# Pair sums from the third block, the short block added to a pair, and a new ScalarE order at the start: one change to a fused four-layer graph network

## The chip, the cores and the metric

The kernel runs on one core of one Trainium2 chip. The metric is the device time of one execution in microseconds; the time given for a kernel is the median of its runs. A change of about 0.2% (6.5 us) is what a measurement of this kernel can tell from no change.

## The reference, cut to what matters

Four graph layers run one after the other on 2708 nodes with 512 features, each with a residual and a layer norm. The change touches layer 0 and the beginning of layer 1:

```python
# layer 0: N = 2708, H = 4 heads of D = 128; both masks are the same adj here
Xw = einsum('hnd,hde->hne', Xh, W)                 # values
f1 = einsum('hnd,hd->hn', Xw, V[:, 0, :, 0]); f2 = einsum('hnd,hd->hn', Xw, V[:, 1, :, 0])
sig = sigmoid(f1[:, :, None] + f2[:, None, :])
att = masked_softmax(adj * sig, adj != 0)          # per row, per head
Xn  = batchnorm(att @ Xw)                          # first attention pass
emb = batchnorm(elu(Xn @ enc_W.T + b) + Xn)
Y   = elu((att @ emb) @ W.T)                       # second attention pass
out = batchnorm(elu(Y @ dec_W.T + b) + Y)
x = layernorm(x + out)
# layer 1
hidden = x @ W1 + b1
x = layernorm(x + (adj != 0) @ hidden / deg)
```

## The kernel before, in words

The nodes are cut into `NT` = 22 blocks of 128 rows; the last one has 20. Python code builds the program once; a tile framework puts the instructions of each engine (TensorE is PE in the profile, VectorE DVE, ScalarE ACT, GpSimd POOL, SyncE SP) into one list, in the order of their priorities and of the framework's own estimate of when each can start. `tc.issue_after(ins)` gives the instructions under it a place behind `ins` in that order. On the chip each engine works through its list in order, and semaphores hold an instruction until its inputs and its buffer are ready. DMAs are issued by SP (`nc.sync`), POOL (`nc.gpsimd`) and ACT (`nc.scalar`), each in the order of its list too.

**First attention pass** (`attention_pass` with `first=True`). Two halves of the columns (`HSPAN`, 1354 each) and two pairs of heads give four sets, here called set 0 (half 0, heads 0 and 1), set 1 (half 0, heads 2 and 3), set 2 and set 3 (half 1). In each set the 22 blocks come in the order `ORDER`: 0 to 10, then the short block of 20 rows at place 11, then the other ten. "Block 9" below is the block at place 9 of its set. For each block `form` makes the attention numerators of both heads in one tile `t` of 128 x 2 x 1354:

- `L400` (ACT): tanh of one head's scores, twice; sigmoid is (1 + tanh)/2.
- `L408` (DVE): add and multiply with the mask tile `a`, both heads in one instruction ("the mask").
- `L409` (ACT): exp of both heads.
- `L491` (PE): twelve products of `t` with the values `xw` into six PSUM tiles `po`.
- `L524` (PE): sums of the rows with a tile of ones into `psm`, eight products.

In sets 0 and 2 (`prepare`) the mask tile is also made from the raw adjacency (`L391`, `L392` on DVE) and stored to DRAM as `adj_d` (`L396`, issued by POOL). Some blocks' `t` are stored too, for the second pass (`L473`, POOL, 1354 KB): blocks 4, 8, 11, 14 and 18 of sets 0 and 2, and eight blocks of sets 1 and 3. There are four buffers for `t` and four for `a`, so the tanh of block k + 4 waits for the products (and the store, if any) of block k.

In sets 1 and 3 the row sums are taken of pairs: for the places from `ALONE` = 4 to 19 the even block waits, and at the odd one DVE adds both (`L517`, one add per head, into the tiles tagged `z` and `pair`), so that one group of eight `L524` products serves two blocks. Places 0 to 3, 20 and 21 are alone. The short block at place 11 is paired with block 10 by adding its rows into the first 20 rows of block 10's own `t` (`L509`), which block 10's `L491` products read.

At the end of a set `keep` copies `po` out and sends the row sums through DRAM; the eight `scaled` steps it returns (multiply `L634` and `bn_stats` `L635` each) are issued one per place in the next set, from place 4 on.

**From layer 0 to layer 1.** `decode` ends with the last decoder products (`ps_dec`, `L893`). Meanwhile `centre` has loaded `w1` and the first five of six column chunks of `xT` into the tile `xs`, and subtracted the mean from `w1` in place. Then the batch norm's scale and shift are found (`ready`), DVE copies `w1` out of `xs` (`L1037`) and clears the last block of `hid_hi` (`L1027`), SP loads the sixth chunk into the place where `w1` was, and for each chunk of `CHUNKS` (450 or 452 columns) ACT scales each of the four feature groups (`L1044`) and DVE adds `xT` (`L1051`). For every block of 128 columns that is complete PE makes a transpose (`tp_out`, `L1057`) and the product with `w1` (`ps_hid`, in `L128`).

Of the kernel before, what the change touches and what calls it, by code (L numbers as in the profile page):

```python
# [8 lines left out]
F32 = mybir.dt.float32  # L9
# [8 lines left out]
P = 128  # L18
# [11 lines left out]
def gnn_stack_kernel(  # L30
# [110 lines left out]
    CHUNKS = [(h0 + q0, w) for (h0, _), ch in zip(HSPAN, HCH) for q0, w in ch]  # L141
    NCH = len(CHUNKS)

    SQ = 4
    SW = 2 * ((HW + 2 * SQ - 1) // (2 * SQ))
    SCH = [[(q * SW, min(SW, w - q * SW)) for q in range(SQ)] for _, w in HSPAN]
# [5 lines left out]

    ORDER = list(range(NT // 2)) + [NT - 1] + list(range(NT // 2, NT - 1))

    ALONE, LAST = 4, 2

# [15 lines left out]
    with ExitStack() as l0:  # L174
# [33 lines left out]
        xT_sb = feat_tile("xT_sb")  # L208

        def load_mlp(w, name):  # L210
            t = p0.tile([P, C, F], F32, tag="mlp_w", name=name)
            nc.sync.dma_start(t, w.rearrange("(c p) o -> p c o", p=P))
            return t

        def project(att, psum):

            held = p0.tile([P, C, F], F32, tag="mlp_w", name="held").rearrange("p c f -> p (c f)")
            w0x = held[:, : H * (P + 2)].rearrange("p (h e) -> p h e", h=H)  # L220
            v12 = att.tile([P, H, 2], F32, tag="v12", name="v12", bufs=1)
            nc.sync.dma_start(v12[:, :, 1], v2.rearrange("(h e) -> e h", h=H))
# [115 lines left out]
        def attention_pass(values, first, att, psum, finish, f1b=None, blocks=(), spread=None, rest=None, taken={}):  # L338
# [23 lines left out]
            def form(hf, p, jt, att, prepare, f1b, tv):  # L362

                h0, w = HSPAN[hf]
                j0, n = BLOCKS[jt]
                src = adjT if prepare else adj_d
                if prepare and hf == 0 and jt < len(blocks):
                    a = blocks[jt]
                else:
                    a = att.tile([P, HW], F32, tag="a", name="a", bufs=4 if first else 3)  # L370

                    early = prepare and hf == 0 and jt < len(blocks) + 2
                    with tc.issue_after(spread.ins) if early else nullcontext():
                        loads.append(
                            nc.sync.dma_start(a[:n, :w], src[j0 : j0 + n, h0 : h0 + w])
                        )
                if n < P:

                    for r in range(HB):
                        if r > 0:  # L380
                            nc.sync.dma_start(
                                a[r * Q : r * Q + n, :w], src[j0 : j0 + n, h0 : h0 + w]
                            )
                        if r + 1 < HB:
                            nc.sync.dma_start(
                                a[r * Q + n : (r + 1) * Q, :w], src[: Q - n, h0 : h0 + w]
                            )
                    n = HR
                if prepare:
                    z = att.tile([P, HW], F32, tag="z", name="z", bufs=1)  # L390
                    nc.vector.tensor_scalar(z[:n, :w], a[:n, :w], 0.0, None, ALU.is_equal)  # L391
                    nc.vector.scalar_tensor_tensor(  # L392
                        a[:n, :w], z[:n, :w], -BIG, a[:n, :w], ALU.mult, ALU.add
                    )
                    m = BLOCKS[jt][1]
                    nc.gpsimd.dma_start(adj_d[j0 : j0 + m, h0 : h0 + w], a[:m, :w])  # L396

                for k in range(HP):
                    h = HP * p + k
                    nc.scalar.activation(  # L400
                        tv[:, k, :],
                        f1b[k][:n, :w],
                        AF.Tanh,
                        bias=f2h[:n, jt, h : h + 1],
                        scale=0.5,
                    )
                ab = a[:n, :w].unsqueeze(1).to_broadcast([n, HP, w])
                step = nc.vector.scalar_tensor_tensor(tv, tv, GUARD, ab, ALU.add, ALU.mult)  # L408
                nc.scalar.activation(tv, tv, AF.Exp, scale=0.5)  # L409
                if not first and p == (jt in KEPT[0]):  # L410

                    with tc.issue_after(step.ins):
                        count(hf, jt, att, a)
                return step
# [5 lines left out]

            later = []
            loads = []
            po = None
            for hf, (h0, w) in enumerate(HSPAN):
                for p in range(H // HP):
# [26 lines left out]
                    for place, jt in enumerate(ORDER):  # L452
# [48 lines left out]

                        if prepare or not ALONE <= place < NT - LAST:
                            whole, m = [t[:, k, :] for k in range(HP)], n
                        elif place % 2 == 0:
                            before = t
                            continue
                        elif n < P:
                            whole, m = [before[:, k, :] for k in range(HP)], P
                            nc.vector.tensor_tensor(  # L509
                                before[:n, :, :w], before[:n, :, :w], tv, ALU.add  # L510
                            )
                        else:

                            whole, m = [], P
                            for k, tag in enumerate(("z", "pair")):
# [2 lines left out]
                                    both[:, :w], before[:, k, :w], tv[:, k, :], ALU.add  # L518
                                )
                                whole.append(both)  # L520
                        for k in range(HP):
                            for r, (q0, qw) in enumerate(SCH[hf]):

# [69 lines left out]
        with (  # L593
# [8 lines left out]
            def keep(hf, p, po, sums):  # L602
# [11 lines left out]
                if not final:  # L614
# [12 lines left out]
                    nc.sync.dma_start(rs_d[part].rearrange(wide).rearrange(cut, s=SR), few)  # L627
                    rb = spread_sums(att, hf, p)

                    def scaled(k, r):  # L630
                        h = HP * p + k
                        q0, qw = SCH[hf][r]
                        dst = ft[:, h, h0 + q0 : h0 + q0 + qw]
                        nc.vector.tensor_tensor(dst, dst, rb[:, k, q0 : q0 + qw], ALU.mult)  # L634
                        nc.vector.bn_stats(stats[:, h, SQ * hf + r, :], dst)  # L635

                    return [
                        lambda k=k, r=r: scaled(k, r) for k in range(HP) for r in range(SQ)
                    ]

                sel = att.tile([P, HW], F32, tag="a", name="sel", bufs=4)
# [59 lines left out]
        with (  # L701
# [104 lines left out]
            def centre(pm):  # L806
# [7 lines left out]
                    xs.rearrange("p t f -> p (t f)")[:, C * c0 : C * (c0 + w)].rearrange(  # L814
                        "p (c j) -> p c j", c=C
                    )
                    for c0, w in CHUNKS
                ]
                for ci in early:
                    load_x(x_held, ci)  # L820
# [9 lines left out]


            held1 = {}
            early = [ci for ci, (c0, w) in enumerate(CHUNKS) if C * (c0 + w) <= (NT - C) * F]

            def load_x(x_held, ci):
                c0, w = CHUNKS[ci]
                nc.sync.dma_start(
                    x_held[ci], xT[:, c0 : c0 + w].rearrange("(c p) j -> p c j", p=P)
                )

            def decode(hf, p, po, rb):
# [145 lines left out]
                wk_again = rest[0][:, : C * F].rearrange("p (c o) -> p c o", c=C)  # L987
                wq_again = rest[1][:, : C * P].rearrange("p (c o) -> p c o", c=C)
                mqk = rest[1][:, C * P : C * P + F]
                nc.sync.dma_start(wk_again, wkT_d)  # L990
                nc.sync.dma_start(wq_again, wqT_d)
                with tc.issue_after(last_dec[0].ins):
# [18 lines left out]
        nc.vector.reciprocal(rdeg, dsum)  # L1011
        scale3, mean3 = batch_scale(stats, MG_DEC, "bn3")
        shift3 = batch_shift(scale3, mean3, MBETA_DEC, "bn3")
        xs, w1_held, x_held = held1["xs"], held1["w1"], held1["x"]

    with (
# [4 lines left out]
        hid_hi = p1.tile([P, NT, F], F32R, name="hid_hi")  # L1023
        hid_lo = p1.tile([P, NT, F], F32R, name="hid_lo")

        with tc.issue_after(ready[0].ins):
            nc.vector.memset(hid_hi[:, NT - 1, :].bitcast(F32), 0.0)  # L1027

# [1 line left out]
        work = main.enter_context(tc.tile_pool(name="l1w", bufs=2))  # L1032
        with tc.tile_pool(name="l1a", bufs=1) as pre:
            b1_sb = load_row(pre, b1, "b1_sb")
            w1_sb = pre.tile([P, C, F], F32, name="w1_sb")
            with tc.issue_after(ready[0].ins):
                nc.vector.tensor_copy(w1_sb, w1_held)  # L1037
            for ci in range(len(early), NCH):
                load_x(x_held, ci)
            turned = 0  # L1040
            for ci, (c0, w) in enumerate(CHUNKS):
                for c in range(C):
                    cols = ot[:, c, c0 : c0 + w]
                    nc.scalar.activation(  # L1044
# [775 lines left out]
```

## Time and profile before

| | |
|---|---|
| time, median of 3 runs | 3248.69 us (3248.22 to 3251.64) |
| the profiled execution's own time | 3254.93 us |
| its span, first to last instruction | 3253.1 us |
| busy: PE, DVE, ACT, POOL | 99%, 59%, 41%, 4% of the span |
| first attention pass (first `po` to the last) | 42.40 to 556.5 us |
| second attention pass begins | 671.9 us |
| last decoder products of layer 0 end | about 1168 us |
| first `ps_hid` of layer 1 | 1173.65 us |
| costliest groups: L408 DVE, L400 ACT, L491 PE (with `xw`), L409 ACT | 444.5, 411.4, 415.1, 367.5 us busy |

Busy times are shares of the whole span and hide what a stage waits for. A busy PE is modelled from the starts of matmuls, so its idle times and the granted clock (1.00 is full, 0.50 is half) tell more than its share. In a timeline row the numbers are the start, the time taken, the engine, the line, what is written and read, and in brackets the idle time of the engine before it and who ended that.

### The profile page before, as it was taken

To read this page: it belongs to the slowest core of one execution; us is meant where nothing else is said; L and a number is where in the kernel's file an instruction comes from. 1 tells how busy PE (TensorE), PEld (TensorE's weight loads), DVE (VectorE), ACT (ScalarE), POOL (GpSimd) and SP (SyncE) were. 2 spreads that over 40 slices of the span, in tenths; PEclk is the share of its full clock that TensorE was granted. 3 is DMA by queue.
4 is the path that set the end of the run, shared out by engine and by line. 5 is a ranking of instruction groups with operands and counts; after the bars stand their busy time and mean duration, and the time that the engine had idled before them with its cause. 6 is when DMAs were issued, how large, how long until landed. Compare 5 with 4: busy or idle time off the path is not lost.

```text
span 3253.1 us, 30379 instructions
## 1 busy us (share of the span) xinstructions
PE 3210.1 (99%) x10906; PEld 1718.6 (53%) x10906; DVE 1924.7 (59%) x3152; ACT 1317.7 (41%) x1494; POOL 136.3 (4%) x219
## 2 busy tenths in 40 slices
PE   8999999999999999999999999999999999999999
PEld 5444444444444446875555555554555555555554
DVE  7888977767686684444145667776353342542433
ACT  6888886567767552001133434443011020120211
POOL 1100100000000000000010000000000000000000
PEclk9999999999999999999999999999999999999999
DMA  8867764346545413540044444553211111111100
GB/s 286 309 214 256 278 243 157 112 141 242 189 165 202 169 47 97 142 126 8 1 135 127 123 127 136 151 159 103 73 47 32 45 36 35 43 32 46 34 24 20
DMA packets 175030, 399.32 MB, mean 123 GB/s; under 512 B 21242, under 2 KB 115910, under 8 KB 168670
## 3 DMA queue, kind: packets, MB, share of 16 engines
q1 hardware_dynamic: 157950, 314.59, 31.5%
q0 software_dynamic: 16496, 80.70, 6.5%
q8 instruction: 86, 1.41, 0.2%
q10 hardware_dynamic: 432, 2.08, 0.2%
q14 instruction: 66, 0.54, 0.0%
HBM read 315.46 MB, written 81.30 MB: 122 GB/s over the span
## 4 chain that ended last, share of the span: by engine, by line
PE 83%; issue 9%; DVE 3%; ACT 2%; DMA 1%; POOL 1%; SPq 0%; POOLq 0%; DVEq 0%; ACTq 0%
PE po L1385 23%; PE ps_s L1264 18%; PE po L491 15%; PE ps_nb L1117 7%; PE ps_wide L1166 4%; PE ps_hid L128 2%; PE ps_sup L1562 2%; PE ps_o L1493 2%; PE ps_dec L893 2%; PE ps_mlp L768 1%; PE psm L524 1%; ACT t L400 1%; ACT t L409 1%; PE ps_s L1256 1%; DVE t L408 1%
## 5 line engine op out<-in xcount | busy, mean ns | idle before, releaser
L408 DVE SCALAR_TENSOR_TENSOR t<-t,a 128x2708 f32<-128x2708 f32 (+1 forms) x150 | 444.5, 2975 | 154.1 <-ACT t L400 149.4
L400 ACT ACTIVATE t<-f1b,f2h 128x1354 f32<-128x1354 f32 (+1 forms) x300 | 411.4, 1413 | 65.6 <-PE po L491 33.3
L491 PE MATMUL po<-t,xw 128*128 128x452 f32 (+3 forms) x1056 | 415.1, 557 | 7.2 <-ACT t L409 7.2
L1264 PE MATMUL ps_s<-sup,hT 128*128 128x384 f32 (+1 forms) x1176 | 407.4, 490 | 0.0
L1385 PE MATMUL po<-sup,e 128*128 128x512 f32 x882 | 407.1, 595 | 0.0
L409 ACT ACTIVATE t<-t 128x2708 f32<-128x2708 f32 (+1 forms) x150 | 367.5, 2454 | 95.8 <-DVE t L408 95.6
L1385 PE MATMUL po<-e,xs 128*128 128x384 f32 (+1 forms) x1176 | 406.0, 489 | 0.0
L491 PE MATMUL po<-t,emb 128*128 128x452 f32 (+3 forms) x1056 | 397.1, 545 | 3.8 <-ACT t L409 3.8
L1696 DVE SCALAR_TENSOR_TENSOR e<-a_cols,ps_s 128x384 f32<-128x384 f32 (+1 forms) x154 | 85.5, 555 | 451.0 <-PE ps_s L1264 428.0
L1264 PEld LDWEIGHTS ps_s<-sup,hT 128*128 128x128 f32 x1176 | 221.8, 190 | 164.2 <-issue 14.2
L491 PEld LDWEIGHTS po<-t,xw 128*128 128x128 f32 (+1 forms) x1056 | 191.0, 192 | 220.0 <-issue 195.6
L1385 PEld LDWEIGHTS po<-e,xs 128*128 128x128 f32 x1176 | 222.2, 190 | 160.2 <-issue 5.8
L491 PEld LDWEIGHTS po<-t,emb 128*128 128x128 f32 (+1 forms) x1056 | 193.6, 190 | 200.3 <-issue 192.1
L1385 PEld LDWEIGHTS po<-sup,e 128*128 128x128 f32 x882 | 160.4, 190 | 159.6 <-issue 136.9
L1264 PE MATMUL ps_s<-hT 128*128 128x384 f32 (+5 forms) x672 | 211.1, 461 | 0.9 <-ACT sup L1569 0.7
L1363 ACT ACTIVATE e<-e 128x384 f32<-128x384 f32 (+1 forms) x308 | 151.7, 522 | 115.0 <-DVE e L1362 111.7
L1611 ACT ACTIVATE a_cols<-a_cols,neg_big 128x384 f32<-128x384 f32 (+1 forms) x154 | 94.6, 616 | 226.5 <-DMA a_cols<-in_adjT_dram 188.2
L1117 PE MATMUL ps_nb<-hid_hi,at 128*128 128x512 f32 x484 | 185.6, 390 | 0.4 <-DVE at L1109 0.4
L1117 PE MATMUL ps_nb<-hid_lo,at 128*128 128x512 f32 x462 | 180.1, 390 | 0.0
L1362 DVE TENSOR_TENSOR e<-e,nmax 128x384 f32<-128x384 f32 (+1 forms) x308 | 162.6, 549 | 23.3 <-ACT nmax L1355 23.3
L108 ACT ACTIVATE ln_rstd<-ln_rstd 128x1 f32<-128x1 f32 (+1 forms) x88 | 17.3, 201 | 392.8 <-DVE ln_rstd L107 392.3
L1264 PEld LDWEIGHTS ps_s<-hT 128*128 128x128 f32 x672 | 123.1, 190 | 89.4 <-issue 20.5
(254 smaller groups left out, 3322.5 us busy)
## 6 DMA issues: line engine op xcount, KB each, us to landing
a<-adj_d SPq DMA_DIRECT2D x108, 677.0 KB
a_cols<-in_adjT_dram SPq DMA_DIRECT2D x378, 192.0 KB
kept<-t POOLq DMA_DIRECT2D x22, 1354.0 KB, 7.3
t<-kept SPq DMA_DIRECT2D x22, 1354.0 KB
a<-in_adjT_dram SPq DMA_DIRECT2D x42, 677.0 KB
adj_d<-a POOLq DMA_DIRECT2D x42, 677.0 KB, 6.0
raw<-in_adjT_dram SPq DMA_DIRECT2D x105, 256.0 KB
a_cols<-in_adjT_dram SPq DMA_DIRECT2D x63, 202.0 KB
```

Source lines behind the costliest of these rows:

```text
L400: nc.scalar.activation(tv[:, k, :], f1b[k][:n, :w], AF.Tanh, bias=f2h[:n, jt, h : h + 1], scale=0.5,)
L408: step = nc.vector.scalar_tensor_tensor(tv, tv, GUARD, ab, ALU.add, ALU.mult)
L409: nc.scalar.activation(tv, tv, AF.Exp, scale=0.5)
L491: nc.tensor.matmul(po[HB * k + q][:, :qw], values[r : r + n, jt, h * P : (h + 1) * P], t[r : r + n, k, q0 : q0 + qw], start=(place == 0), ...
L1117: nc.tensor.matmul(pos[it][:n], at, half[:, jt, :], start=(jt == 0 and k == 0), stop=(jt == NT - 1),)
L1166: nc.tensor.matmul(ps[:, :width], w(c, o), xt(c), start=(c == 0), stop=(c == C - 1),)
L1264: nc.tensor.matmul(ps[:, b * P : w], keys[:, c, j0 : j0 + P], st["q"][:, c, b * P :], start=(c == 0), stop=(c == C - 1),)
L1362: nc.vector.tensor_tensor(e, e, st["nmax"][:, :w], ALU.add)
L1363: nc.scalar.activation(e, e, AF.Exp)
L1385: nc.tensor.matmul(out, lhsT, rhs, start=(k == 0), stop=(k == NT - 1))
L1611: nc.scalar.activation(a, a, AF.Identity, bias=neg_big[: a.shape[0]], scale=1.0e30)
L1696: nc.vector.scalar_tensor_tensor(e, a, 2.0, ps, ALU.mult, ALU.add)
```

## The change

In seven places, all in layer 0 and at the start of layer 1:

1. `ALONE` goes from 4 to 3, so pairs begin at place 3 and blocks 9 and 10 form a pair of their own. The short block at place 11 is added, by one add per head, into the first 20 rows of that pair's sum tiles, and the group's products come then.
2. In the first set, the tanh of the blocks 1 to 4 are put behind a given instruction: those of block 1 behind the last tanh of block 0, those of blocks 2, 3 and 4 behind the exp of blocks 0, 1 and 2.
3. The eight `scaled` steps become sixteen: multiply and `bn_stats` are separate.
4. The pool of the tag `mlp_w` changes from `p0` to `pf`, which stays open until layer 1's inputs are made.
5. `w1` is brought out of `xs` by a DMA from SP behind the last decoder product, into the buffer of `dec_w`, instead of by DVE.
6. The memset of `hid_hi`'s last block is on POOL.
7. The first column chunk is cut into 128 and 324 columns (`PIECES`), for the loads of `xT` and for layer 1's start.

```diff
+    PIECES = [(0, P), (P, CHUNKS[0][1] - P)] + CHUNKS[1:]
...
-    ALONE, LAST = 4, 2
+    ALONE, LAST = 3, 2
+    assert ORDER.index(NT - 1) % 2 == ALONE % 2 == NT % 2 + 1
...
         def load_mlp(w, name):
-            t = p0.tile([P, C, F], F32, tag="mlp_w", name=name)
+            t = pf.tile([P, C, F], F32, tag="mlp_w", name=name)
...
-            held = p0.tile([P, C, F], F32, tag="mlp_w", name="held").rearrange("p c f -> p (c f)")
+            held = pf.tile([P, C, F], F32, tag="mlp_w", name="held").rearrange("p c f -> p (c f)")
...
+                turn = opening.get(jt) if prepare and hf == 0 else None
                 for k in range(HP):
                     h = HP * p + k
-                    nc.scalar.activation(
-                        tv[:, k, :],
-                        f1b[k][:n, :w],
-                        AF.Tanh,
-                        bias=f2h[:n, jt, h : h + 1],
-                        scale=0.5,
-                    )
+                    with tc.issue_after(turn.ins) if turn else nullcontext():
+                        tanh = nc.scalar.activation(
+                            tv[:, k, :],
+                            f1b[k][:n, :w],
+                            AF.Tanh,
+                            bias=f2h[:n, jt, h : h + 1],
+                            scale=0.5,
+                        )
                 ab = a[:n, :w].unsqueeze(1).to_broadcast([n, HP, w])
                 step = nc.vector.scalar_tensor_tensor(tv, tv, GUARD, ab, ALU.add, ALU.mult)
-                nc.scalar.activation(tv, tv, AF.Exp, scale=0.5)
+                exp = nc.scalar.activation(tv, tv, AF.Exp, scale=0.5)
+                if not opening:
+                    opening[1] = tanh
+                if len(opening) < 4:
+                    opening[len(opening) + 1] = exp
...
+            opening = {}
...
                         if prepare or not ALONE <= place < NT - LAST:
                             whole, m = [t[:, k, :] for k in range(HP)], n
-                        elif place % 2 == 0:
+                        elif n < P:
+                            m = P
+                            for k in range(HP):
+                                nc.vector.tensor_tensor(
+                                    whole[k][:n, :w], whole[k][:n, :w], tv[:, k, :], ALU.add
+                                )
+                        elif before is None:
                             before = t
                             continue
-                        elif n < P:
-                            whole, m = [before[:, k, :] for k in range(HP)], P
-                            nc.vector.tensor_tensor(
-                                before[:n, :, :w], before[:n, :, :w], tv, ALU.add
-                            )
                         else:
...
                                 whole.append(both)
+                            before = None
+                            if BLOCKS[ORDER[place + 1]][1] < P:
+                                continue
...
-                    def scaled(k, r):
+                    def scaled(k, r, counted):
...
-                        nc.vector.tensor_tensor(dst, dst, rb[:, k, q0 : q0 + qw], ALU.mult)
-                        nc.vector.bn_stats(stats[:, h, SQ * hf + r, :], dst)
+                        if not counted:
+                            nc.vector.tensor_tensor(dst, dst, rb[:, k, q0 : q0 + qw], ALU.mult)
+                        else:
+                            nc.vector.bn_stats(stats[:, h, SQ * hf + r, :], dst)
...
+                w1_sb = pf.tile([P, C, F], F32, tag="mlp_w", name="w1_sb")
+                with tc.issue_after(last_dec[0].ins):
+                    nc.sync.dma_start(w1_sb, held1["w1"])
+                held1["w1"] = w1_sb
                 nc.sync.dma_start(wk_again, wkT_d)
...
-        with tc.issue_after(ready[0].ins):
-            nc.vector.memset(hid_hi[:, NT - 1, :].bitcast(F32), 0.0)
+        nc.gpsimd.memset(hid_hi[:, NT - 1, :].bitcast(F32), 0.0)
...
-            w1_sb = pre.tile([P, C, F], F32, name="w1_sb")
-            with tc.issue_after(ready[0].ins):
-                nc.vector.tensor_copy(w1_sb, w1_held)
-            for ci in range(len(early), NCH):
+            for ci in range(len(early), len(PIECES)):
                 load_x(x_held, ci)
             turned = 0
-            for ci, (c0, w) in enumerate(CHUNKS):
+            for ci, (c0, w) in enumerate(PIECES):
```

(The two other loops over `CHUNKS` that serve these loads, in `x_held` and `early`, run over `PIECES` as well.)

## The prediction

> **What bounds the kernel now.** I read the page first, then a table by stage, then the timelines of the engines at the places where the stages lose time.
>
> ```profile
> span 3253.1 us, 30379 instructions
> PE 3210.1 (99%) x10906; PEld 1718.6 (53%) x10906; DVE 1924.7 (59%) x3152; ACT 1317.7 (41%) x1494; POOL 136.3 (4%) x219
> ...
> core 0: us, PE busy (x) PEld busy (x) DVE busy (x) ACT busy (x) POOL busy (x), PEclk, DMA share, GB/s
> 42.40:171.98 129.58, 129.58 (x617) 55.99 (x616) 117.78 (x71) 111.18 (x67) 18.03 (x31) 1.00 0.82 289
> 171.98:294.15 122.17, 120.00 (x492) 53.48 (x489) 101.85 (x62) 109.63 (x68) 6.22 (x11) 0.99 0.66 233
> 294.15:432.92 138.77, 134.67 (x620) 57.86 (x617) 122.84 (x89) 115.73 (x70) 15.76 (x28) 0.96 0.79 279
> 432.92:556.50 123.58, 119.79 (x492) 53.91 (x488) 93.89 (x65) 101.12 (x62) 4.93 (x9) 0.99 0.54 189
> ```
>
> TensorE sets the end, so I ask only where it waits or runs slowly. The four rows are sets 0 to 3 of the first attention pass. With no wait an alone block takes 6.03 us (42.40 to 48.43 in the timeline), a pair 10.58 (4.66 and 5.92), and the 20-row block with its sums 2.99. Set 0 is 21 x 6.03 + 2.99 = 129.6: nothing is lost. Sets 1 and 3 should take 117.9 and lose 4.2 and 5.7; set 2 should take 129.6 and loses 9.2. So 19 us lie open in this pass. Where:
>
> ```profile
> 235.77 2.49 PE L524 MATMUL psm<-t,ones 128*32 128x340 f32 x16 [1.41 <-DVE t L509]
> ...
> 357.88 6.51 PE L491 MATMUL po<-t,xw 128*128 128x452 f32 x12 [2.20 <-ACT t L409]
> ...
> 369.62 7.83 PE L491 MATMUL po<-t,xw 128*128 128x452 f32 x12 [0.96 <-ACT t L409]
> ...
> 511.02 9.16 PE L491 MATMUL po<-t,xw 128*128 128x452 f32 x19 [2.38 <-ACT t L409]
> ...
> core 0: us, PE busy (x), PEclk, DMA share, GB/s
> 235.80:239.21 3.41, 3.41 (x18) 0.50 0.02 5
> 358.68:362.09 3.41, 3.41 (x6) 0.50 0.82 278
> 368.92:375.75 6.83, 6.12 (x8) 0.50 0.94 320
> ```
>
> The bracket is TensorE's idle time and who ended it. The second table shows that after such waits the granted clock is 0.50 for 3.41 us or twice that, so a wait also costs up to 1.7 or 3.4 us of slow matmuls.
>
> The wait of 357.88 begins on POOL's queue:
>
> ```profile
> 343.88 0.53 POOL L396 DMA_DIRECT2D adj_d<-a  x1 [5.45 <-DVE a L392]
> 344.40 0.53 POOL L473 DMA_DIRECT2D kept<-t  x1
> ```
>
> The 1354 KB store of block 8's `t` goes out right behind the 677 KB store of `a` and lands 9.5 us later (the DMA issues of this window). The tanh of block 12 needs that buffer and stands ahead of block 10's exp on ScalarE (4.67 us idle there).
>
> The opening and the start of layer 1:
>
> ```profile
> 30.24 8.00 ACT L400 ACTIVATE t<-f1b,f2h 128x1354 f32<-128x1354 f32 x6 [1.71 <-DMA f1b<-f_d]
> 38.14 2.44 ACT L409 ACTIVATE t<-t 128x2708 f32<-128x2708 f32 x1
> ...
> 34.33 2.98 DVE L408 SCALAR_TENSOR_TENSOR t<-t,a 128x2708 f32<-128x2708 f32 x1 [1.85 <-ACT t L400]
> ...
> 1171.37 1.34 PE L1057 MATMUL tp_out<-ident,ot 128*128 128x128 f32 x4 [3.40 <-DVE ot L1051]
> 1173.65 2.08 PE L128 MATMUL ps_hid<-w_sb,ot 128*128 128x512 f32 x2 [0.93 <-DVE w_sb L1037]
> ```
>
> Six tanh run before the first exp, and the first mask (L408) waits for the third, since the two heads of block 0 stand first and third. Layer 1's first product waits for the copy of `w1`.
>
> **The change, part by part** (by the changed program's own instruction order).
>
> *Opening.* ScalarE's list becomes tanh 0,0,1,1, exp 0, tanh 2,2, exp 1, instead of 0,1,0,1,2,2, exp 0. The mask of block 0 starts one tanh (1.32 us, 7.90/6) earlier. The chain of waits there runs 34.33 mask, 37.31 copies on VectorE, 38.12 pxw on TensorE, 40.23 copy, 42.40 first `po`; all of it moves by 1.3 us. Exp 0 could start 2.1 us earlier, but it is not on that chain. A gain of **1.3** (0 if ScalarE's later waits eat it, 2.3 if TensorE's slow stretch at 38 us goes too). From block 5 on, set 0's lists are the old ones; its exps reach TensorE just in time (108.67 for 108.71), so nothing more.
>
> *Pairs from place 3.* In sets 1 and 3 one group of eight sum matmuls goes: 6.03 - 4.66 = 1.37 us on TensorE, twice, **2.7**. VectorE gets two more full adds of 1.48 us a set; it is busy 102 and 94 us of 122 and 124, so they hide.
>
> *The short block.* Before, L509 adds block 11 into block 10's `t`: it waits for block 10's matmuls, runs 2.97 us, and TensorE's sums wait (1.41 us in each set). Now blocks 9 and 10 are paired first and block 11 is added into the pair (two adds of about 1.5 us, the L517 duration at the same width). That wait goes. What is late next: the masks of blocks 12, 13 and 14 are queued behind these adds on VectorE, and the adds wait for exp 11. Worked from P(9), the time that TensorE takes block 9: blocks 11 and 12 are due at +9.3 and +12.4. Exp 11 can end at +5.3 (the tanh of block 12 ahead of it needs block 8's buffer), the adds end at +8.6, mask 12 at +11.5, and exp 12 near +13.9 (ahead of it on ScalarE stands a tanh of block 14 that needs block 10's buffer, free at +9.3). So a new wait of 1.5 us (0.7 to 3) at block 12, in both sets. Will it slow the clock? The Trainium skill, "TensorE: Matmul & The Clock Gate", section "HAM oscillation", says that no idle gap over about 3.4 us is the rule to keep. By the rule a wait of 1.5 us costs itself alone, and the waits removed here (1.41 to 2.38 us) would also give back themselves alone. The trace speaks otherwise: each of the four waits above has a stretch at 0.50 beside it (only set 3's wait for L509, at 496.71, has none). I take the trace: 0.6 x 1.7 = 1.0 beside each new wait. Sets 1 and 3 then lose 2.5 each instead of 4.2 and 5.7: a gain of **4.9**. By the rule only idle time counts: 1.41 + 0.75 and 1.41 + 2.38 go, twice 1.5 comes, 3.0 in all.
>
> *Halved `scaled` steps.* Nothing is removed; multiply (0.50) and bn_stats (0.50) become two steps. In set 2 the built order still gives each block one of each, 5.98 us of VectorE in a block of 6.03; only the crowd around block 5 thins, by two steps (0.84 us). That covers most of the 0.65 and 0.28 us waits (blocks 5 and 6, at 325.12 and 331.50): **1.0**.
>
> *POOL's queue in set 2.* Moved as a consequence: block 8's store now stands ahead of the store of `a` and should land in 5 to 6 us (a store issued ahead of one took 6.0 at 318.54, 5.1 at 382.94). Needed: about 6.9 us after exp 8 (two tanh and exp 10 follow). So the wait of 2.20, its slow clock, and part of what follows go. The wait of 0.96 at block 12 stays, as tanh 14 still stands ahead of exp 12. But block 4's store has moved behind a store of `a`: it may land at 326.3, when both had landed before; block 6's exp allows 326.6. I count 5.5 of the 8.0 us lost from block 10 to 13 (0 to 7): **5.5**.
>
> *Layer 1.* The first chunk is cut at 128 columns, so ScalarE's four scalings take about 0.4 us each instead of 0.65, and the first transpose comes near 1170.6 instead of 1171.4. The copy of 1.16 and the memset of 0.48 leave VectorE. In their place SP issues a 1024 KB DMA of `w1` after the last decode product (1164.4): the nearest row is `wk_again`, 1024 KB, 5.1 us (1124.86 to 1129.94), so it lands near 1170, 1172 at the latest, while TensorE wants it at 1170.9. Behind it in SP's queue wait the `mqk_d` store (due 1168.6 anyway), the last chunk of `xT` (before at 1173.6) and `b1` (needed 4 us later): none late. POOL's memset (bounds 0.5 to 2, no row of this size) meets an idle POOL. The stage is then 3.87 us of TensorE per block with no idle, so what its start gains stays: between 0.8 and 4.3 (the slow stretch of 1171.05 to 1177.88 gone too). I take **2.6**. The moved `mlp_w` pool costs nothing: the second attention pass has the same instructions in the same order on all engines.
>
> Sum: 1.3 + 2.7 + 4.9 + 1.0 + 5.5 + 2.6 = 18.0. The profiled execution took 3254.9 us (span 3253.1 and 1.8 around it), 6.2 above the median of 3248.7. So 3236.9 in its own time, **3231** against the median.
>
> **The rivals.**
> *The store's wait moves (0.22).* Block 4's store, now second, or block 8's again, lands 9.5 us late, and set 2 loses its 8 us as before: the gain is about 11 us, 3238. For it: 10 us stores in set 0 too (87.34 to 97.39).
> *No new waits, no slow clock (0.08).* The allowances at block 12 and layer 1 vanish: 24 to 28 us, about 3222.
> *Hidden (0.06).* ScalarE, busy 109.6 of 122.2 us in set 1, becomes the bound of sets 1 and 3, and only the opening and layer 1 remain: 4 us, 3245.
> *Late stores make it slower (0.04).* ScalarE's order puts a tanh that waits for a store ahead of an exp that is ready. Set 2 has four large stores; each that lands more than about 7 us after its exp costs up to the 8 us of block 8's. Without set 2 the gain is 11.5; set 2's loss was 9.2, so two late stores still gain and from three on the kernel is slower: 3253 with three, 3261 with four. Against it: only one of four was late before.
>
> **How the numbers follow.** The likeliest case has 0.60 and by itself spans 3225 to 3237. The range 3219 to 3241 takes in most of the moved wait and of the lucky case. About 0.2% (6.5 us) is what a measurement of this kernel can tell from no change: below 3242.2 is faster. The first three cases give 0.90, hidden 0.06, slower 0.04.
>
> **What would show it.** The first `po` at 41.1 instead of 42.4; sets 1 and 3 at 119 instead of 122.2 and 123.6, with no wait for an add of 20 rows at the sums of block 11 but one of 1 to 2 us at block 12; set 2 near 132; no 4.7 us idle on ScalarE for `kept`; the first `ps_hid` near 1171 on the old time axis, less the gains ahead. A `kept` wait at block 6 or 10 of set 2, or longer waits at block 12, would prove me wrong, as would a late `w1` DMA.

## The result, and the profile after

The changed kernel takes 3236.49 us (median of 5 runs, 3232.57 to 3239.3), the kernel before 3249.62 in the same session: a ratio of 0.9956 (95% interval 0.9945 to 0.9968), or 13.1 us less. In another session, in experiment e2, the ratio was 0.9953 (0.9941 to 0.9966). The profiled execution took 3233.64 us (span 3231.8). The two profiles lie 21.3 us apart, the medians only 13.1; the profile of before lies 5.3 us above its median here, the one after 2.9 below. Where these 8 us went is the first thing that the experiments settle.

The table by stage of the changed kernel, with its four sets in the order of before (from a set's first `po` to the next set's):

```profile
core 0: us, PE busy (x) PEld busy (x) DVE busy (x) ACT busy (x) POOL busy (x), PEclk, DMA share, GB/s
43.38:173.29 129.91, 129.91 (x618) 56.20 (x617) 116.73 (x71) 113.26 (x68) 18.02 (x31) 1.00 0.82 292
173.29:290.76 117.47, 116.54 (x477) 52.86 (x473) 104.74 (x66) 109.15 (x68) 6.20 (x11) 1.00 0.69 239
290.76:423.33 132.57, 129.72 (x621) 56.01 (x617) 122.15 (x88) 114.89 (x70) 15.71 (x28) 1.00 0.80 283
423.33:540.42 117.09, 116.16 (x475) 52.87 (x472) 95.93 (x67) 101.16 (x62) 4.92 (x9) 1.00 0.60 209
```

Sets 1 and 3 have come down to 117.5 and 117.1, further than the 119 forecast, and set 2 to 132.6, which is the forecast. But the first `po` comes at 43.38, not at 41.1. The end of set 3 is the start of its last sum product, here and in all that follows; in the profile of before that is 556.12, so that its set 3 took 123.2 us, where the prediction's table goes on to 556.50. TensorE's waits in these sets, from its timeline:

```profile
236.40 5.95 PE L503 MATMUL po<-t,xw 128*128 128x452 f32 x15 [0.93 <-ACT t L416]
...
328.88 3.30 PE L503 MATMUL po<-t,xw 128*128 128x452 f32 x8 [1.89 <-ACT t L416]
...
363.05 3.30 PE L503 MATMUL po<-t,xw 128*128 128x452 f32 x8 [0.96 <-ACT t L416]
...
486.44 4.06 PE L503 MATMUL po<-t,xw 128*128 128x452 f32 x10 [0.93 <-ACT t L416]
```

The waits for the 20-row add are gone; block 12 waits 0.93 us in sets 1 and 3. The wait of 2.20 at block 10 of set 2 is gone too, but block 6 has a new one of 1.89. ScalarE and POOL show whose it is:

```profile
325.06 1.43 ACT L407 ACTIVATE t<-f1b,f2h 128x1354 f32<-128x1354 f32 x1 [3.00 <-DMA kept<-t]
```

```profile
315.24 0.53 POOL L400 DMA_DIRECT2D adj_d<-a  x1 [8.28 <-DVE a L396]
315.76 0.53 POOL L485 DMA_DIRECT2D kept<-t  x1
...
339.18 0.53 POOL L485 DMA_DIRECT2D kept<-t  x1 [5.48 <-ACT t L416]
339.70 0.53 POOL L400 DMA_DIRECT2D adj_d<-a  x1
```

Block 4's store now goes out behind a store of `a` and lands at 324.95, 9.2 us later; block 8's goes ahead of one and lands after 6.4 us. This is the event that the prediction named as the moved wait. The opening, on ScalarE:

```profile
30.48 1.42 ACT L407 ACTIVATE t<-f1b,f2h 128x1354 f32<-128x1354 f32 x1 [2.14 <-DMA f1b<-f_d]
32.77 4.05 ACT L407 ACTIVATE t<-f1b,f2h 128x1354 f32<-128x1354 f32 x3 [0.86 <-DMA f1b<-f_d]
37.24 2.46 ACT L416 ACTIVATE t<-t 128x2708 f32<-128x2708 f32 x1 [0.42 <-DVE t L415]
```

The second tanh now is head 1's, and it waits 0.86 us for the second `f1b`. Before, block 1's tanh of head 0 stood there and covered this landing. The first `po` is later than in the profile of before (42.40) because the clock stayed at 0.50 for 6.83 us from 37.26, where before it did so for 3.41; in e2, with 3.41, the first `po` came at 41.90. And the start of layer 1, on TensorE:

```profile
1152.97 0.33 PE L1079 MATMUL tp_out<-ident,ot 128*128 128x128 f32 x1 [2.79 <-DVE ot L1073]
1153.13 1.62 PE L128 MATMUL ps_hid<-w_sb,ot 128*128 128x512 f32 x2
```

The first product follows the first transpose at once; there is no wait for `w1` (issued at 1146.78). From the start of the last decoder product to the first `ps_nb` the stage takes 93.9 us instead of 96.8. (In the profile of before the decoder products end at 1164.5; what ends near 1168 there are the products of `wk_again` and `wq_again`, L994.)

### The profile page after: what moved, and what is told of

Same layout as the page of the kernel before. It is cut to its first block, busy times and chain, and to the rows that moved or that the text cites. A ratio compares the mean times of both kernels' runs of the same rounds, so it can differ in the third digit from the quotient of the medians.

```text
span 3231.8 us, 30335 instructions
## 1 busy us (share of the span) xinstructions
PE 3196.0 (99%) x10874; PEld 1714.4 (53%) x10874; DVE 1929.0 (60%) x3160; ACT 1318.2 (41%) x1498; POOL 136.1 (4%) x220
## 4 chain that ended last, share of the span: by engine, by line
PE 85%; issue 8%; DVE 3%; ACT 2%; DMA 1%; POOL 1%; SPq 0%; POOLq 0%; DVEq 0%; ACTq 0%
PE po L1407 24%; PE ps_s L1286 18%; PE po L503 16%; PE ps_nb L1139 7%; PE ps_wide L1188 5%; PE ps_hid L128 2%; PE ps_sup L1584 2%; PE ps_o L1515 2%; PE ps_dec L914 2%; PE ps_mlp L789 1%; PE psm L540 1%; PE ps_s L1278 1%; ACT t L416 1%; PE tp L1178 1%; DVE t L415 1%
## 5 line engine op out<-in xcount | busy, mean ns | idle before, releaser
L503 PE MATMUL po<-t,xw 128*128 128x452 f32 (+3 forms) x1056 | 407.6, 549 | 4.7 <-ACT t L416 4.7
L1286 PEld LDWEIGHTS ps_s<-hT 128*128 128x128 f32 x672 | 123.2, 190 | 89.3 <-issue 20.8
```

What stands on the lines that cost most here:

```text
L503: nc.tensor.matmul(po[HB * k + q][:, :qw], values[r : r + n, jt, h * P : (h + 1) * P], t[r : r + n, k, q0 : q0 + qw], start=(place == 0), ...
L1286: nc.tensor.matmul(ps[:, b * P : w], keys[:, c, j0 : j0 + P], st["q"][:, c, b * P :], start=(c == 0), stop=(c == C - 1),)
```

## The experiments

Ratios are to the kernel before in the same session, with 95% intervals; the gain in us is worked out from the ratio and that session's median of before. In all profiles together I measured the stages by the same marks.

**e1, the kernel before once more; e2, the changed kernel once more** (no edit).

> The kernel before once more, to see what of its profile belongs to the program and what to one execution. Between the two profiles 21.3 us lie, between the medians 13.1. Of the 21.3, 10.3 are idle time and matmuls removed (TensorE's waits sum to 36.9 and 29.3 us, and two groups of sums go, 2.7), the rest is the granted clock (eight stretches at 0.50 before, three after). Theory 'tied' (my prediction's): a slow stretch follows a wait; then the waits of sets 1 to 3 (1.41, 0.75, 2.20, 0.96, 1.41, 2.38) come back, four of them or more with a stretch at 0.50 beside them, and the span is again near 3253. Rival 'loose': the waits come back to within 0.1 us, since the program sets them, but the stretches are at other places or missing; the span may be anywhere from 3244 to 3253, and set 1 takes 120 and set 2 133 to 135 where no stretch falls into them. The time is 3249.6 plus or minus 2 in both.

> The changed kernel once more. Both theories: 3236.5 plus or minus 3, with waits of 0.93 at block 12 of sets 1 and 3, 0.96 at block 12 of set 2, and the wait for the stored t at block 6 of set 2 (1.89). First po near 43.4 if the slow stretch of the opening (6.83 us from 37.26) comes back, near 42.3 if it is 3.41 long as before. 'Tied': slow stretches only beside waits of 1.4 us or more, so none in sets 1 and 3 again. 'Loose': one to three stretches at places that the first profile of this kernel did not have, each costing 1.7 us.

e1: 3247.96 us, ratio 1.0001 (0.9993 to 1.001). e2: 3232.37 us, 0.9953 (0.9941 to 0.9966), a gain of 15.3 (11.0 to 19.2). The sets of e1, by stage (sets 0 to 3):

```profile
42.37:172.15 129.78, 129.76 (x618) 56.10 (x617) 117.25 (x71) 111.19 (x67) 18.01 (x31) 1.00 0.81 289
172.15:295.74 123.59, 119.80 (x493) 53.82 (x489) 102.92 (x64) 109.86 (x68) 6.21 (x11) 0.99 0.65 231
295.74:428.04 132.30, 131.34 (x621) 56.73 (x617) 121.83 (x87) 115.21 (x70) 15.73 (x28) 0.99 0.82 291
428.04:551.24 123.20, 119.41 (x492) 53.85 (x488) 93.51 (x64) 101.11 (x62) 4.92 (x9) 0.99 0.54 189
```

Set 2 takes 132.30 us, not 138.77: block 8's store, in the same place of the same queue, landed 7.0 us after its issue instead of 9.5, and TensorE did not wait at block 10. Of the 6.5 us between the two profiles in this set, 3.1 are idle time (4.09 against 0.96; the waits of 0.65 and 0.28 at blocks 5 and 6 are gone as well) and 3.4 are slow clock (10.24 us at 0.50 against 3.41). So the largest loss that I had read off the profile belonged to that one execution. Neither theory had this: both expected the 2.20 back. The span is 3246.3 against 3253.1, and set 2's 6.5 us are nearly all of it. The slow stretches had moved as "loose" says: beside block 14 of set 1 (a wait of 2.37 this time) and not beside the 20-row add.

In e2 block 4's store again went second and landed 9.6 us later; block 6 waited 0.74. Set 2 took 131.4, sets 1 and 3 117.8 and 117.1.

**e3, the halved steps alone; e4, the pairs alone; e5, the layer 1 parts alone** (each on the kernel before; the hunks are those of the change and only their marks are shown: e4 has the new branches for the short block too, e5 all of parts 4 to 7).

```diff
# e3
-                    def scaled(k, r):
+                    def scaled(k, r, counted):
...
# e4
-    ALONE, LAST = 4, 2
+    ALONE, LAST = 3, 2
...
# e5
+                w1_sb = pf.tile([P, C, F], F32, tag="mlp_w", name="w1_sb")
...
```

> The kernel before with part 3 alone (sixteen scaled steps instead of eight). In the built order this part alone moves POOL's queue in set 2: block 8's store ahead of the store of a, block 4's behind one. My prediction's terms: 1.0 for the halved steps and 5.5 for the queue, 6.5 in all: 3243. What the profile of the changed kernel shows in set 2: the wait of 2.20 at block 10 gone, a new one of 1.89 at block 6, 0.96 at block 12 as before, blocks 5's 0.65 and 6's 0.28 gone, so by idle time alone 1.2 us (3248.4). 'Tied' adds the slow clock that went with block 10's wait but must charge one to block 6's: 3 to 6 us. 'Loose': 1 to 2 us. Sets 1 and 3 as before (waits for the 20-row add of 1.41).

> The kernel before with part 1 alone (pairs from place 3, the short block added to the pair). My prediction: 2.7 for two groups of sums and 4.9 for the waits, 7.6: 3242. By idle time alone: 2.7 + (2 x 1.41 + 0.75 + 2.38 - 2 x 0.93) = 6.8, 3242.8. By the stages of the two profiles: sets 1 and 3 shorter by 4.7 and 6.1, 10.8, 3238.8 ('tied'). In the profile: sets 1 and 3 at 117.5, no wait for a 20-row add, 0.93 at block 12 of both; set 2 as before with its 2.20 at block 10, since POOL's order is the old one.

> The kernel before with parts 4 to 7 alone (the layer 1 parts). My prediction: 2.6. All six profiles so far have this stage the same to 0.1 us: from the last decoder product to the first ps_nb 96.8 us with the old form and 93.9 with the new, so 2.9 whatever happens elsewhere: 0.9991 of before. Of it 1.7 is the second half of a slow stretch (6.83 us long with the old form, 3.41 with the new), the rest 0.6 at the first tp_out and the wait of 0.93 for w1. Rival: moving the pool of dec_w and w1 changes the first pass or the second too; then set times or the second pass differ from 129.6, 122, 132 to 138, 122 and 435.4.

e3: 3248.57, ratio 1.0002 (0.9994 to 1.001): nothing gained, where the prediction had 6.5. In the profile set 2 took 138.0, and block 4's store, now behind a store of `a`, landed 11.6 us after its issue:

```profile
333.54 7.67 PE L491 MATMUL po<-t,xw 128*128 128x452 f32 x12 [3.04 <-ACT t L409]
```

e4: 3243.39, 0.9982 (0.9975 to 0.9989), a gain of 5.8 (3.6 to 8.1) against 7.6 forecast. Sets 1 and 3 took 118.8 and 120.1, not 117.5, because block 12 waits 2.24 us there:

```profile
231.47 2.74 ACT L402 ACTIVATE t<-f1b,f2h 128x1354 f32<-128x1354 f32 x2 [0.50 <-PE po L493]
234.12 2.44 ACT L411 ACTIVATE t<-t 128x2708 f32<-128x2708 f32 x1
```

With whole `scaled` steps two tanh of block 14 (the x2) stand ahead of block 12's exp on ScalarE. The changed kernel has one there; its exp begins at 233.90, with the products due at 235.5:

```profile
232.57 1.43 ACT L407 ACTIVATE t<-f1b,f2h 128x1354 f32<-128x1354 f32 x1 [1.20 <-PE po L503]
233.90 2.45 ACT L416 ACTIVATE t<-t 128x2708 f32<-128x2708 f32 x1
```

In e4 these two waits are equal, and yet set 3 took 1.3 us longer than set 1: a stretch at 0.50 followed the wait in set 3 (from 488.65), and none in set 1.

e5: 3246.91, 0.9994 (0.9986 to 1.0002), a gain of 1.9 (-0.6 to 4.5), which the medians alone cannot tell from none. The stage took 93.9 us, as in the changed kernel; the first pass kept its times (129.6, 122.0, 132.9, 123.2).

**e9, pairs and halved steps together; e10, the changed kernel with whole `scaled` steps** (e9 is e3's and e4's hunks together, e10 the change without e3's).

```diff
# e10, against the changed kernel
-                    def scaled(k, r, counted):
+                    def scaled(k, r):
...
```

> The kernel before with parts 1 and 3 together, with the lists of ScalarE and POOL in sets 1 to 3 the same as in the changed kernel. Alone the pairs gave 5.8 us (3.6 to 8.1) and the halved steps -0.6 (-3.2 to 2.0). Theory 'together': with whole scaled steps the pairs have two tanh of block 14 ahead of block 12's exp (a wait of 2.24 in sets 1 and 3, with a slow stretch in one of them), with halved steps only one (0.93). Then both parts give more than the sum: sets 1 and 3 at 117.5 and 117.1 against 122.0 and 123.2 of before, about 10.5, less 1 to 2 us for block 4's store in set 2: 9 to 10 us below before (0.9970). Rival 'sum': 5.2 us (0.9984), with waits of 2 us at block 12 as with the pairs alone; the rest of the whole change's 13 to 16 us then comes from layer 1 and the opening.

> The changed kernel without part 3 (scaled steps whole, so POOL's old order in set 2). Theory 'together': the wait at block 12 of sets 1 and 3 is 2.24 again, sets 1 and 3 take 118.8 to 120.5 as with the pairs alone; set 2 132.3 or, if block 8's store lands over 9 us late, 138; 5 to 6 us slower than the changed kernel, about 9 to 10 below before (0.9970). Rival 'sum': no loss against the changed kernel (0.995 to 0.9957), or a gain of 1 us since block 4's store goes first.

e9: 3238.28, 0.9968 (0.9956 to 0.998), a gain of 10.4 (6.5 to 14.3). The two parts alone sum to 5.2; together they give about twice that, with sets 1 and 3 at 117.5 and 117.1 and a wait of 0.92 at block 12. Block 4's store landed in time (7.5 us), so set 2's 132.5 held no wait for it. e10: 3238.92, 0.9968 (0.9956 to 0.9981), a gain of 10.4 (6.2 to 14.3), and the wait is back in both sets (set 1's is shown):

```profile
234.87 5.58 PE L503 MATMUL po<-t,xw 128*128 128x452 f32 x14 [2.24 <-ACT t L416]
```

Sets 1 and 3 took 118.8 and 120.1 again. So the halved steps are worth 1.3 and 3.0 us in sets 1 and 3 (one slow stretch in it), and only beside the pairs (alone, in e3, they left sets 1 and 3 at 121.9 and 121.7 with the old waits of 1.41). The intervals of the gains overlap, so the medians alone leave "together" and "sum" open; the rows decide for "together", since the wait at block 12 goes from 2.24 to 0.92 with the halved steps (e4 to e9) and comes back without them (e10).

**e6, every store of `t` ahead of the store of `a` beside it; e8, block 14's tanh behind block 12's exp in every set** (both on the changed kernel).

```diff
# e6
-                    nc.gpsimd.dma_start(adj_d[j0 : j0 + m, h0 : h0 + w], a[:m, :w])
+                    with tc.issue_after(stored[0].ins) if stored else nullcontext():
+                        nc.gpsimd.dma_start(adj_d[j0 : j0 + m, h0 : h0 + w], a[:m, :w])
+                    stored.clear()
...
-                                nc.gpsimd.dma_start(kept[:n, :, :w], tv)
+                                stored[:] = [nc.gpsimd.dma_start(kept[:n, :, :w], tv)]
...
# e8
+                if first and ORDER.index(jt) == 14:
+                    turn = opening["12"]
...
+                if ORDER.index(jt) == 12:
+                    opening["12"] = exp
```

> The changed kernel with every 1354 KB store of t put ahead of the 677 KB store of a that is issued beside it (sets 0 and 2). In six profiles block 4's store in set 2 landed 6.0 to 7.9 us after its issue where it went first, and 9.2 to 11.6 where it went second, and the late ones cost 0.74, 1.89 and 3.04 at block 6. Theory 'order': both stores of set 2 now land in 5 to 8 us, no wait for a stored t in set 2, only the 0.96 at block 12; set 2 takes 130.6 to 131 (132.6 and 131.4 in the changed kernel): 0.7 to 2 us less than the changed kernel, that is 14 to 17 us (0.9948 to 0.9957) below the kernel before. Rival 'chance': landing times vary for other reasons (the load of all queues), and a wait of 0.7 to 3 us at block 6 or 10 is seen again.

> The changed kernel with the tanh of block 14 behind the exp of block 12 on ScalarE in every set (in the changed kernel one tanh of block 14 stands ahead of that exp in sets 1, 2 and 3 and waits for block 10's products). By the rows of the changed kernel in set 1: mask 12 ends at 233.37 and the exp began at 233.90, so the exp gains 0.5 and the wait of 0.93 at block 12 shrinks to 0.4; in set 2 the exp stands ready while the tanh waits, and most of the 0.96 goes. Theory 'ScalarE's order': 1.5 to 2 us less than the changed kernel in sets 1 to 3 together. Rival 'VectorE': the masks behind the short adds are what is late, and then the wait stays at 0.9 in sets 1 and 3, or moves on to block 13 or 14, whose tanh is now one exp later: no gain or up to 1.5 us slower.

e6: 3233.48, 0.9955 (0.9941 to 0.9969). Both large stores of set 2's first half landed in 6.8 us and nothing waited for them; but set 2 took 132.5, because a wait of 1.15 at block 12 was followed by a stretch at 0.50. This is what "order" expects, and e11 has it again (7.5 and 7.4 us), but stores that went second landed in time as well in e7 and e9 (7.8 and 7.5), so two profiles do not exclude "chance". The time of the whole kernel doesn't show it.

e8: 3238.61, 0.9969 (0.9957 to 0.998), a gain of 10.1 (6.5 to 14.0), where e6 and e7, which leave sets 1 and 3 as they are, had 14.6 and 14.0 in that session. Set 2 gained (129.9, no wait at block 12), but sets 1 and 3 took 120.7 and 121.3: a wait came at block 14, whose tanh is now late, and in set 3 block 12 still waits (set 3 shown), as the rival said:

```profile
487.30 9.37 PE L507 MATMUL po<-t,xw 128*128 128x452 f32 x24 [1.41 <-ACT t L418]
...
499.88 2.38 PE L507 MATMUL po<-t,xw 128*128 128x452 f32 x4 [1.94 <-ACT t L418]
```

**e7, TensorE's wait ahead of layer 1 filled** (on the changed kernel; the added products are read by nobody).

```diff
+                with tc.issue_after(last_dec[0].ins):
+                    for o in range(3):
+                        nc.tensor.matmul(
+                            po[0], wq_again[:, o, :], wk_again[:, o, :], start=(o == 0), stop=(o == 2)
+                        )
```

> The changed kernel with three products more (1.3 us each by the row of the mqk products, 0.43 us per pass and two passes a product, 2.6 in all), whose result nobody reads, in TensorE's wait of 2.79 us ahead of layer 1's first transpose. In all six profiles the slow stretches lie on a grid of 3.413 us; a stretch follows each grid window with 2.0 us or more of idle TensorE and none with up to 1.17 us (unless the 20-row products lie in it); with 1.26 to 1.72 both occur. Theory 'window': with the wait filled to 0.2 us the stretch at 1150 disappears, the first ps_hid to the first ps_nb take 85.3 instead of 86.98, 1.7 us less: about 15 to 17 below before. Rival: the half clock there has another cause (the load of DMAs that begins at 1151, or a new kind of work); then the stretch stays and the time is that of the changed kernel. It would be slower if tp_out waited for the added products.

3234.59, 0.9957 (0.9944 to 0.9969). TensorE there, and the clock of the stretches that begin with the wait's end:

```profile
1149.84 2.74 PE L1029 MATMUL po<-wk_again,wq_again 128*128 128x512 f32 x6
1152.89 0.62 PE L1084 MATMUL tp_out<-ident,ot 128*128 128x128 f32 x2 [0.31 <-DVE ot L1078]
...
1169.53 0.66 PE L1084 MATMUL tp_out<-ident,ot 128*128 128x128 f32 x4 [0.56 <-ACT xs L1091]
```

```profile
1150.90:1154.30 3.40, 3.09 (x9) 1.11 (x8) 1.99 (x9) 2.56 (x7) 0.53 (x1) 1.00 0.75 210
1154.30:1157.70 3.40, 3.40 (x14) 1.85 (x13) 3.08 (x10) 3.40 (x7) 0.00 (x0) 1.00 0.96 273
```

The clock stays at 1.00, where the changed kernel's first 3.41 us of layer 1 ran at 0.50. So the idle time was what made it slow: the loads and the kind of work, which the rival named, are the same in both. But only 0.4 us came of it (93.5 for 93.9), not 1.7. The first `ps_hid` comes 0.4 us later behind the last decoder product than in the changed kernel, and from there to the first `ps_nb` 0.8 us are gained (86.14 for 86.98), since the faster products run into a wait for ScalarE a few blocks later (0.56 at 1169.53).

**e11, set 2 mended** (the changed kernel with e6, e7, and e8's rule in set 2 alone).

```diff
+                if prepare and hf == 1 and ORDER.index(jt) == 14:
+                    turn = opening["12"]
...
```

> The changed kernel with three edits that the runs point to: every store of t ahead of the store of a beside it; block 14's tanh behind block 12's exp in set 2 alone (in sets 1 and 3 it cost 3 to 4 us each); the filled wait ahead of layer 1. From the rows: set 2 at 129.7 to 129.9 (no wait for a store, none at block 12) instead of 131.4 to 132.6, and 0.4 at layer 1: 2 to 3 us below the changed kernel, 16 to 18 below before (0.9945 to 0.995). Rival: the two edits of set 2 together give a new order on ScalarE or POOL with a wait elsewhere in the set, or the slow stretches of the rest of the kernel hide it: the time of the changed kernel.

3234.71, 0.9954 (0.9941 to 0.9966): no better than the changed kernel by what can be told (0.9956 and 0.9953). Set 2 and the stretch after its short block:

```profile
289.58:421.11 131.53, 131.30 (x621) 56.74 (x617) 122.12 (x88) 115.50 (x70) 15.70 (x28) 0.99 0.83 291
...
359.10:362.50 3.40, 3.32 (x5) 1.66 (x6) 3.35 (x2) 3.40 (x4) 0.54 (x1) 0.50 0.91 300
```

TensorE hardly waits any more in this set (131.30 busy of 131.53), yet 3.4 us at half clock follow the 20-row products and take back what the waits gave.

## Why the prediction was nearly right in its number, and wrong in its parts

It said 3231 and a gain of 18.0; the runs gave 13.1 and, in e2, 15.3. Its direction and most of its mechanisms held. Two terms were off by 6.5 and 3.8 us in opposite directions, and that they nearly cancel is luck: the number says little for the parts. By the stages the gain is 11.4 in sets 1 and 3, 2.9 at layer 1 and 0.3 at the opening, 14.6 together, with nothing from set 2 that can be told; the two measured gains lie on either side of it.

- **POOL's queue in set 2 (5.5) and the halved steps there (1.0): the step that failed.** I took set 2's loss in one profile for the program's. Five profiles have the old order of the stores (before, e1, e4, e5, e10): 138.8, 132.3, 132.3, 132.9 and 132.4. Block 8's store landed 9.5 us after its issue in the first and in 7.0 to 8.6 in the others: the late store is one case in five. With the changed order (changed kernel, e2, e3, e7, e9) set 2 took 132.6, 131.4, 138.0, 130.6 and 132.5: again one in five with a loss of this size, now at block 6, and against the usual case nothing that can be told is gained. And the profile had said so: it was 6.2 us above its median. I wrote this down and then took 6.5 off for a loss that the median didn't hold.
- **"The store's wait moves" was a rival at 0.22, and half of it is what happened in set 2**: in both profiles of the changed kernel TensorE waited at block 6 for block 4's store (1.89 and 0.74, landings of 9.2 and 9.6 us), but set 2 did not lose its 8 us by it; only e3 shows that (138.0). Over all profiles block 4's store landed in 6.0 to 8.8 us going first (seven), and in 7.5 to 11.6 going second (six).
- **Pairs from place 3 (2.7) and the short block (4.9): 7.6 forecast, 11.4 found, with the halved steps in it** (sets 1 and 3 together: 245.4 and 246.8 in the two profiles of before, 234.6 and 234.9 in the two after). Without them, in e4, it is 238.9, so 7.2 from the pairs: near the forecast, but with waits of 2.24 where 1.5 had been forecast. The 2.7 is as worked out: one group of sums goes in each set. The loss of set 3 to begin with was 5.3, not 5.7 (the mark at its end, see above). In the changed kernel the new wait came where it was forecast, at block 12 for the exp behind the tanh of block 14, but was 0.92 or 0.93 (once 1.27) instead of 1.5, and no slow stretch followed it in six profiles with this order (the changed kernel, e2, e6, e7, e9, e11), where I had charged 1.0 for each.
- **The halved steps were put in the wrong place.** Their gain is not in block 5 of set 2 but in sets 1 and 3, 4.3 us by e4 against the changed kernel: they keep the second tanh of block 14 behind block 12's exp. I read this order off the changed program without seeing which part had made it.
- **Opening (1.3): 0.2 to 0.3.** In the seven profiles with the new order the mask of block 0 begins at 34.15 on average, in six with the old one at 34.43; the first `po` at 42.5 and 42.7. Single profiles scatter more than that (33.45 to 34.65). The second `f1b` lands at 32.0 to 33.1 and the tanh of head 1 waits for it. I had asked what the mask waits for, but not what its tanh would wait for once it came earlier.
- **Layer 1 (2.6): 2.9 in every profile with these parts alone** (3.1 and 3.3 with the filled wait). The first transpose gained 0.6 (0.8 forecast), the wait for `w1` is gone, the slow stretch fell from 6.83 to 3.41, and POOL's memset took 0.52 on an idle engine.
- **Not in the sum:** the second pass took 433.9 in both profiles of the changed kernel and 435.4 in both of before (435.39 and 435.48), for one slow stretch. e9 has 433.9 without the layer 1 parts, and e7, e8 and e10, with them, have 436.8, 435.6 and 435.4, so the difference is not bound to the change.
- **The Trainium skill's rule and the trace**: I took the trace, a price of 1.7 us beside a wait of 1.4 to 2.4, against the rule that only gaps over about 3.4 us count. Neither was the whole of it. Gaps far below 3.4 us did slow the clock (2.20 in the profile of before), so the rule is too mild here; but a wait of 1.4 to 2.4 had no price of its own either (2.24 in set 1 of e4). And one of the four stretches did not come from the wait beside it: the one at 368.92 began when the wait that ended at 369.62 was only 0.3 us old, behind a piece with the 20-row products in it and 0.25 us of idle time. What counts is the idle time in a piece of the clock's grid (below).

## What to carry to other kernels

Before a loss in a profile is counted as a gain, set the profiled time against the median: a wait that ends on a DMA's landing, in a profile that is slower than its median by as much, may be an accident of that execution; a second profile of the same kernel tells. When an instruction is pulled forward, ask what its own inputs are waiting for, not only what it releases. And parts of a change that touch the same engine's order are worth measuring together and apart: here two of them gave 5.8 and nothing alone, and 10.4 as a pair, and the rows of the profile showed why where the intervals could not.

## What the runs showed of the hardware

The slow stretches follow a rule that is sharper than I had expected. In each of the 13 profiles all stretches at 0.50 after the first 25 us begin on one grid of 3.413 us, to within 5 ns (the Trainium skill, "TensorE: Matmul & The Clock Gate", section "What's actually happening", has a free-running window of 3413 ns). I cut every trace after 25 us into these pieces and summed TensorE's idle time in each, leaving aside pieces already at 0.50 and pieces that hold over 1 us of the 20-row products. All 43 pieces with 1.94 to 3.35 us idle are followed by a stretch at 0.50; of the some 11,900 with 1.78 or less, none is. Once at 0.50, less is enough to stay there: 12 pieces already slow had 0.71 to 1.43 us idle and a second slow one followed, and with 0.51 or less none did. Layer 1 fits this: it began with 6.83 us at 0.50 in all five profiles in which TensorE waited 0.93 for `w1` inside the first slow piece, and with 3.41 (or none, with the filled wait) in the eight without. A wait of 3.31 us that fell across two pieces cost nothing, as in the second attention pass of the changed kernel (first two rows), while in the kernel before it fell into one and slowed the next (last two):

```profile
856.50:859.90 3.40, 1.66 (x5) 0.55 (x3) 3.40 (x3) 2.98 (x3) 0.00 (x0) 1.00 0.00 0
859.90:863.30 3.40, 1.83 (x5) 1.05 (x6) 3.40 (x7) 3.40 (x3) 0.00 (x0) 1.00 0.00 0
...
874.08:877.49 3.41, 0.28 (x1) 0.00 (x0) 3.41 (x6) 2.99 (x2) 0.00 (x0) 1.00 0.00 0
877.49:880.90 3.41, 3.23 (x5) 1.59 (x6) 3.41 (x7) 2.77 (x3) 0.00 (x0) 0.50 0.34 102
```

The grid lies differently against the program in each execution, so the same waits cost 1.7 us in one and nothing in the next. The fastest and the slowest run of the changed kernel lie 6.7 us apart, at mean granted clocks of 0.999 and 0.997, which by my estimate from these rounded clocks is about 6 us of a span of 3235; most of the scatter can be this. Pieces with the 20-row products in them go to half clock earlier, in e11 with 0.16 us idle; where the limit lies there these runs do not settle.
